# Order of the last attention group in a fused macaron block: values first, then maximum and weights, and a closing one step later

## The chip, the core and the metric

The kernel runs on one NeuronCore of a Trainium2 chip. The metric is device time in microseconds (us) of one execution; the time of a kernel is the median of its runs. The engines are named as in the profile: PE is TensorE (matmul; PEld its weight loads), DVE is VectorE, ACT is ScalarE, POOL is GpSimd, SP is SyncE. Each engine takes its own instructions in order, and waits on semaphores for the others.

## The reference

The input `x` is 2 x 2048 tokens of 256 numbers, float32. Three sublayers follow each other, each on a layer norm of `x`:

```
x = x + 0.5 * ffn(layernorm(x))
x = x + attn(layernorm(x))
x = x + 0.5 * ffn(layernorm(x))

ffn(x):  silu(q(x) @ q(w_gate).T) * (q(x) @ q(w_up).T)  ->  q(h) @ q(w_down).T      # hidden 704
attn(x): scores = (qr kr + qi ki) / sqrt(256);  softmax;  weights @ vr, weights @ vi;  @ Wo.T + bo
```

`q` rounds to a 4-bit grid in blocks of 16 numbers. The attention has one head; queries, keys and values are 512 wide (a real and an imaginary part of 256).

## The kernel before, in words

The 4096 tokens are 32 tiles of 128. The kernel folds the attention's matrices when it starts (`wa` from Wq and Wk, `wvo` from Wv and Wo), so that scores are a product of normed tokens with `uT = wa * normed tokens`, and the values' product is weights times normed tokens, followed by `wvo`.

**Attention** (`attention`, L660 to L903) works on 8 groups of 4 query tiles (512 queries, `Q`), 4 groups for each of the 2 batches. A group goes through 8 steps (`NP`), each for a pair of key tiles. One loop (L873) counts steps `n` over all groups, and in each step three groups are at work:

- the scores of group `gi` (`scores`, L701): PE writes `ps`, ACT copies it to a piece `st` (128 x 1024), DVE keeps the running maximum `most`; `peak` (L724) turns it on PE (`pm`) and reduces it on DVE to `mx` in the group's last step;
- the weights of the group ahead: `highest` (L734) spreads `mx` over the partitions, with four transposes on PE (`pb`) and a copy on ACT to `top`; `weights` (L741) subtracts `top` from a piece on DVE (L743), takes exp on ACT (L744) and, in the last group, adds the piece to `sums` on POOL (L750, L753);
- the values of the group that is 8 + 2 steps behind (`LAG` is 2): `values` (L776). Groups 0 to 6 use seven half-size products instead of eight: PE writes seven quarters `m` in two PSUM tiles (L805), with right sides that DVE has added up (`tw`, L764 to L768). The last group, number 7, takes the plain way: 4 matmuls of 512 columns a step into `z` (L783).

When a group's values are complete, `totals` (L833) transposes the sums of its weights on PE (`pl`) and takes their reciprocals on DVE (L842, L843); `collect` (L815) puts the seven quarters together into `zT`, with a copy on ACT (L824) and seven adds on DVE (L825 to L831), which also frees the two PSUM tiles of `m`; `close` (L850) multiplies `zT` by `wvo` on PE (`poa`, L856) and adds the result to `x` on DVE (L864). `closing` carries a group from `collect` to a later step's `close`.

**The second FFN** starts while attention ends. It is a generator (`ffn`) of which the loop at L935 takes one turn after some steps of attention, from step 66 on after each. A turn computes a tile's gate and up products (`gu`, L428, 8 matmuls of 352 columns, in PSUM tiles out of the same two buffers `p_big` as the seven quarters `m`), Silu on ACT (L442), and their product on DVE (L446); later turns round the result, transpose it (`th`, L463) and multiply it by the down matrix (`po`, L472).

No order is written out by hand at this place. Each engine's order comes from a planner, which starts from the order in which the code issues and may place an instruction ahead of one that it expects to wait. So a moved call shifts what stands near it, and can change what else is put between.

Steps 64 to 73 of the loop have no scores left: they hold the weights of group 7 (steps 64 to 71), the last two steps of values of group 6 (steps 64 and 65), and the values of group 7 (steps 66 to 73).

Of the kernel before, what the change touches and what calls it, by code (L numbers as in the profile page):

```python
# [52 lines left out]
def kernel(ctx: ExitStack, tc: tile.TileContext, x, wqT, bq, wkT, bk, wvT, bv, woT, bo,  # L53
# [539 lines left out]
    NP = tiles // 2  # L593
    LAG = 2
    RING = NP // 2 + LAG
    groups = NT // QG
# [63 lines left out]
    def attention(batches, at, kt, late):  # L660
# [15 lines left out]
        def queries(gi):  # L676
            gr = Group()
            gr.i = gi
            b, k = divmod(gi, tiles // QG)
            gr.of = batches[b]  # L680
            gr.uT = kt.tile([P, KD, Q], FP, tag="uT", name=f"uT{gi}", bufs=2)
            for c in range(KD):
                ps = p_t.tile([P, 2, HQ], FP, tag="t", name=f"pu{gi}_{c}")
                for h in range(2):
                    for kc in range(KD):
                        nc.tensor.matmul(  # L686
                            out=ps[:, h, :],
                            lhsT=wa[:, kc, ts(c, P)],
                            rhs=gr.of.xT[2 * k + h][:, kc, :, :].rearrange("p v t -> p (v t)"),
                            start=(kc == 0),  # L690
                            stop=(kc == KD - 1),
                        )
                nc.scalar.activation(
                    gr.uT[:, c, :], ps.rearrange("p h q -> p (h q)"), AF.Identity, bias=wkbq[:, c:c + 1]
                )
            gr.rc = at.tile([P, QG], FP, tag="rc", name=f"rcg{gi}", bufs=2)
            nc.vector.tensor_scalar(gr.rc, gr.of.rc[:, ts(k, QG)], bqbk, None, ALU.add)
            gr.pieces = []
            return gr

        def scores(gr, s):  # L701
            n = gr.i * NP + s
            pool = at if n // RING % 2 == 0 else late["pool"]
            piece = pool.tile([P, 2, Q], FP, tag="st", name=f"st{gr.i}_{s}", bufs=RING)
            for v in range(2):
                ps = p_acc.tile([P, Q], FP, tag="acc", name=f"ps{gr.i}_{s}_{v}")
                for c in range(KD):
                    scored = nc.tensor.matmul(  # L708
                        out=ps,
                        lhsT=gr.of.xT[s][:, c, v, :],  # L710
                        rhs=gr.uT[:, c, :],
                        start=(c == 0),
                        stop=(c == KD - 1),
                    )
                nc.scalar.copy(piece[:, v, :], ps)  # L715
                if s == 0 and v == 1:
                    gr.most = at.tile([P, Q], FP, tag="most", name=f"most{gr.i}")
                    seen = nc.vector.tensor_tensor(gr.most, ps, piece[:, 0, :], ALU.max)
                elif s > 0:
                    seen = nc.vector.tensor_tensor(gr.most, ps, gr.most, ALU.max)  # L720
            gr.pieces.append(piece)
            return seen.ins, scored.ins
# [11 lines left out]
        def highest(gr):  # L734
            pt = p_t.tile([P, QG, P], FP, tag="t", name=f"pb{gr.i}")
            for u in range(QG):
                nc.tensor.transpose(pt[:, u, :], gr.mx[:, u:u + 1].to_broadcast([P, P]), ident)
            gr.top = late["pool"].tile([P, Q], FP, tag="top", name=f"top{gr.i}")
            nc.scalar.copy(gr.top, pt.rearrange("p u s -> p (u s)"))  # L739

        def weights(gr, s):  # L741
            piece = gr.pieces[s]
            nc.vector.tensor_tensor(piece, piece, gr.top.unsqueeze(1).to_broadcast([P, 2, Q]), ALU.subtract)  # L743
            nc.scalar.activation(piece, piece, AF.Exp, scale=SCALE)  # L744
            if s == 0:
                gr.sums = late["pool"].tile([P, 2, HQ], FP, tag="sums", name=f"sums{gr.i}")
            if not seven(gr):
                both = piece.rearrange("p v (h q) -> p v h q", h=2)
                if s == 0:
                    add(gr.sums, both[:, 0, :, :], both[:, 1, :, :], ALU.add)  # L750
                else:
                    for v in range(2):
                        add(gr.sums, gr.sums, both[:, v, :, :], ALU.add)  # L753

        def seven(gr):
            return gr.i < groups - 1

        def sums_of_weights(gr, s):


            piece = gr.pieces[s]
            b = piece.rearrange("p v (h q) -> p (v h) q", h=2)
            t = late["pool"].tile([P, 4, HQ], FP, tag="tw", name=f"tw{gr.i}_{s}", bufs=2)
            nc.vector.tensor_tensor(  # L764
                t[:, 0:2, :], b[:, 0:4:3, :], b[:, 1:2, :].to_broadcast([P, 2, HQ]), ALU.add
            )
            nc.vector.tensor_tensor(t[:, 3, :], t[:, 1, :], b[:, 0, :], ALU.add)  # L767
            nc.vector.tensor_tensor(t[:, 2, :], t[:, 3, :], b[:, 2, :], ALU.add)  # L768
            if s == 0:
                gr.first = t  # L770
            else:
                add(gr.sums, t[:, 1:3, :], gr.first[:, 1:3, :] if s == 1 else gr.sums, ALU.add)  # L772
                gr.first = None
            gr.t[s] = t
# [40 lines left out]
        def collect(gr):  # L815
            gr.zT = late["pool"].tile([P, KD, Q], FP, tag="zT", name=f"zT{gr.i}")
            if not seven(gr):
                for c in range(KD):
                    nc.scalar.copy(gr.zT[:, c, :], gr.z[c])  # L819
                return  # L820
            m1, m6, m2, m7, m5, m3, m4 = gr.m
            u = late["pool"].tile([P, 3, HQ], FP, tag="u", name=f"u{gr.i}")
            vadd = nc.vector.tensor_tensor
            nc.scalar.copy(u[:, 0, :], m1)  # L824
            vadd(u[:, 1, :], m6, u[:, 0, :], ALU.add)  # L825
            vadd(gr.zT[:, 0, 0:HQ], m2, u[:, 0, :], ALU.add)
            vadd(u[:, 2, :], m7, u[:, 1, :], ALU.add)
            vadd(gr.zT[:, 1, HQ:Q], m5, u[:, 2, :], ALU.subtract)
            vadd(u[:, 1, :], m5, u[:, 1, :], ALU.subtract)
            vadd(gr.zT[:, 0, HQ:Q], m3, u[:, 1, :], ALU.add)  # L830
            vadd(gr.zT[:, 1, 0:HQ], m4, u[:, 2, :], ALU.add)  # L831
# [13 lines left out]
        def residual(gr):  # L845
            g, j = divmod(gr.i * QG, GT)
            gr.xo = xs[g][:, j:j + QG, :]
            nc.gpsimd.tensor_tensor(gr.xo, gr.xo, bout.unsqueeze(1).to_broadcast([P, QG, D]), ALU.add)

        def close(gr):  # L850
            xo = gr.xo
            for u0 in range(0, QG, 2):
# [10 lines left out]
                for u in range(u0, u0 + 2):  # L863
                    nc.vector.scalar_tensor_tensor(  # L864
                        xo[:, u, :], po[:, u - u0, :], gr.rs[:, u:u + 1], xo[:, u, :], ALU.mult, ALU.add
                    )

        def behind(seen):
            return tc.issue_after(seen) if seen is not None else nullcontext()

        todo = {0: queries(0)}
        closing = None
        for n in range(groups * NP + NP + LAG):  # L873
            gi, s = divmod(n, NP)
            seen, scored = scores(todo[gi], s) if gi < groups else (None, None)
            with behind(seen):
                if s == 0 and 0 < gi <= groups:
                    todo[gi - 1].t = {}
                    highest(todo[gi - 1])
                    weights(todo[gi - 1], 0)  # L880
                if s + 1 < NP and 0 < gi <= groups:
                    weights(todo[gi - 1], s + 1)
                if s == NP // 2 and gi + 1 < groups:
                    todo[gi + 1] = queries(gi + 1)
                gv, sv = divmod(n + 1 - NP - LAG, NP)
                if 0 <= gv < groups and seven(todo[gv]):
                    sums_of_weights(todo[gv], sv)
                if n >= NP + LAG:
                    gv, sv = divmod(n - NP - LAG, NP)
                    values(todo[gv], sv)  # L890
                    if closing is not None:
                        close(closing)
                        closing = None
                    if sv == LAG:
                        residual(todo[gv])
                    if sv == NP - 1:
                        closing = todo.pop(gv)
                        totals(closing)
                        collect(closing)
                if s == NP - 1 and gi < groups:  # L900
                    peak(todo[gi])
            yield seen, scored
# [11 lines left out]
    late = {}  # L914
    batches = [Batch(b) for b in range(NB)]
    att = attention(batches, at, kt, late)
    begun = 0
    done = 0
# [82 lines left out]
```

## Time and profile before

| | us |
|---|---|
| median of 3 runs | 1074.61 (1074.57 to 1074.98) |
| the profiled execution, its own time | 1073.74 |
| its span in the profile | 1071.9 |
| PE busy | 1044.7 (97% of the span) |
| DVE busy | 805.8 (75%) |
| ACT busy | 469.9 (44%) |
| POOL busy | 253.6 (24%) |
| L783, the values of the last group, first to last start | 769.2 to 837.5 |
| granted PE clock | 1.0 |

The profile's times are counted from the start of the span. A row of the timeline has start, duration, engine, line, operation, tiles written and read, sizes, how many instructions are merged in it, and in brackets the idle time of the engine before it and what ended it. A matmul in float32 shows as two rows of PE (x8 for four matmuls); a transpose as one.

### The profile page before, as it was taken

To read this page: it belongs to the slowest core of one execution; us is meant where nothing else is said; L and a number is where in the kernel's file an instruction comes from. 1 tells how busy PE (TensorE), PEld (TensorE's weight loads), DVE (VectorE), ACT (ScalarE), POOL (GpSimd) and SP (SyncE) were. 2 spreads that over 40 slices of the span, in tenths; PEclk is the share of its full clock that TensorE was granted. 3 is DMA by queue.
4 is the path that set the end of the run, shared out by engine and by line. 5 is a ranking of instruction groups with operands and counts; after the bars stand their busy time and mean duration, and the time that the engine had idled before them with its cause. 6 is when DMAs were issued, how large, how long until landed. Compare 5 with 4: busy or idle time off the path is not lost.

```text
span 1071.9 us, 11329 instructions
## 1 busy us (share of the span) xinstructions
PE 1044.7 (97%) x4206; PEld 731.6 (68%) x4206; DVE 805.8 (75%) x1387; ACT 469.9 (44%) x739; POOL 253.6 (24%) x148
## 2 busy tenths in 40 slices
PE   6998999999999999999999999999999999999998
PEld 5676777777775666676675666666655777777776
DVE  7999998867634888576688958678767587777575
ACT  4754654544335735447343633343333244343232
POOL 4563121210103020111124111212461021221110
PEclk9999999999999999999999999999999999999999
DMA  9000000000000000000000000000000000000001
GB/s 321 1 1 1 1 1 1 1 1 1 0 1 1 1 1 0 1 1 1 0 1 1 1 0 1 1 1 1 0 1 1 10 20 10 20 10 20 20 10 40
DMA packets 7286, 13.50 MB, mean 13 GB/s; under 512 B 1344, under 2 KB 3648, under 8 KB 6848
## 3 DMA queue, kind: packets, MB, share of 16 engines
q1 hardware_dynamic: 6128, 12.13, 3.1%
q10 hardware_dynamic: 1104, 0.66, 0.3%
q8 instruction: 33, 0.54, 0.2%
q14 instruction: 21, 0.17, 0.1%
HBM read 8.59 MB, written 4.19 MB: 12 GB/s over the span
## 4 chain that ended last, share of the span: by engine, by line
PE 89%; DVE 7%; ACT 2%; DMA 1%; issue 1%; POOL 0%; SPq 0%; DVEq 0%; ACTq 0%; POOLq 0%
PE gu L428 26%; PE ps L708 19%; PE m L805 15%; PE po L472 14%; PE th L463 4%; PE poa L856 3%; PE pu L686 2%; PE z L783 2%; PE tx L403 1%; DVE st L743 1%; PE wm L338 1%; PE txa L624 1%; ACT xn L234 1%; DVE h L285 1%; DVE h L283 1%
## 5 line engine op out<-in xcount | busy, mean ns | idle before, releaser
L428 PE MATMUL gu<-wgu,xqT 128*128 128x352 f32 x1024 | 317.9, 460 | 3.0 <-DVE h L446 2.7
L428 PEld LDWEIGHTS gu<-wgu,xqT 128*128 128x128 f32 x1024 | 188.4, 190 | 97.6 <-DVE h L446 3.8
L708 PE MATMUL ps<-uT,xT 128*128 128x512 f32 x512 | 232.2, 593 | 0.7 <-DVE most L720 0.7
L472 PE MATMUL po<-wd,hqT 128*128 128x256 f32 x768 | 176.1, 379 | 0.0
L472 PEld LDWEIGHTS po<-wd,hqT 128*128 128x128 f32 x768 | 144.7, 190 | 28.2 <-ACT zT L819 0.6
L708 PEld LDWEIGHTS ps<-uT,xT 128*128 128x128 f32 x512 | 95.1, 190 | 93.2 <-issue 81.0
L720 DVE TENSOR_TENSOR most<-ps,most 128x512 f32<-128x512 f32 x112 | 77.0, 688 | 93.5 <-ACT st L715 92.8
L184 POOL TENSOR_TENSOR h<-h,qh_s 128x1408 f32<-128x1408 f32 x26 | 67.5, 2595 | 294.0 <-DVE h L182 252.1
L715 ACT COPY st<-ps 128x512 f32<-128x512 f32 x128 | 74.5, 583 | 134.1 <-PE ps L708 133.5
L805 PE MATMUL m<-tw,xn 128*128 128x256 f32 x448 | 124.9, 380 | 0.0
L464 ACT COPY hqT<-th 128x512 f32<-128x512 f32 (+1 forms) x128 | 55.4, 481 | 156.7 <-PE th L463 154.5
L772 POOL TENSOR_TENSOR sums<-tw,sums 128x512 f32<-128x512 f32 x42 | 56.9, 1354 | 232.3 <-DVE tw L768 212.9
L744 ACT ACTIVATE st<-st 128x1024 f32<-128x1024 f32 x64 | 67.5, 1057 | 76.0 <-DVE st L743 75.6
L805 PE MATMUL m<-st,xn 128*128 128x256 f32 x336 | 100.0, 379 | 0.0
L446 DVE TENSOR_TENSOR h<-h,gu 128x704 f32<-128x704 f32 x64 | 56.3, 879 | 55.5 <-PE gu L428 52.8
L805 PEld LDWEIGHTS m<-tw,xn 128*128 128x128 f32 x448 | 84.8, 190 | 13.1 <-DVE tw L767 1.2
L743 DVE TENSOR_TENSOR st<-st,top 128x1024 f32<-128x1024 f32 x64 | 83.2, 1312 | 0.8 <-ACT top L739 0.8
L805 PEld LDWEIGHTS m<-st,xn 128*128 128x128 f32 x336 | 63.2, 190 | 26.2 <-issue 19.4
L180 DVE SCALAR_TENSOR_TENSOR h<-qh_m,h 128x1408 f32<-128x1408 f32 (+1 forms) x30 | 45.8, 1527 | 33.1 <-ACT qh_m L179 32.9
L442 ACT ACTIVATE h<-gu 128x704 f32<-128x704 f32 x64 | 48.2, 753 | 44.9 <-PE gu L428 44.6
L179 ACT ACTIVATE qh_m<-h 128x1408 f32<-128x1408 f32 (+1 forms) x30 | 38.9, 1297 | 45.9 <-DVE h L170 42.1
L463 PE MATMUL th<-ident,h 128*128 128x128 f32 x384 | 53.1, 273 | 1.4 <-ACT hqT L464 1.4
(175 smaller groups left out, 1262.5 us busy)
## 6 DMA issues: line engine op xcount, KB each, us to landing
out_dram<-x SPq DMA_DIRECT2D x15, 256.0 KB, 2.1
x<-in_x_dram SPq DMA_DIRECT2D x3, 1024.0 KB, 13.1
n_down<-in_w_down_dram SPq DMA_DIRECT2D x1, 704.0 KB, 9.6
n_up<-in_w_up_dram SPq DMA_DIRECT2D x1, 640.0 KB, 6.2
x<-in_x_dram ACTq DMA_DIRECT2D x1, 512.0 KB, 5.4
wq_sb<-in_wqT_dram SPq DMA_DIRECT2D x1, 512.0 KB, 6.8
wk_sb<-in_wkT_dram SPq DMA_DIRECT2D x1, 512.0 KB, 4.5
wv_sb<-in_wvT_dram SPq DMA_DIRECT2D x1, 512.0 KB, 6.8
```

Source lines behind the costliest of these rows:

```text
L184: last.tensor_tensor(yb, yb, scale.unsqueeze(2).to_broadcast([P, nb, BLK]), ALU.mult)
L428: nc.tensor.matmul(out=ps[:, b2, 0:HALF], lhsT=xqT[:, i % XT, kc, :], rhs=wgu[:, kc, ts(which * 2 + b2, HALF)], start=(kc == 0), stop=(kc ...
L446: nc.vector.tensor_tensor(h, h, up, ALU.mult)
L463: nc.tensor.transpose(ps[:, r - r0, :], hq[:, chunk(r)], ident)
L472: nc.tensor.matmul(out=po, lhsT=hqT[:, r, :], rhs=wd[:, r, :], start=(r == 0), stop=(r == NR - 1))
L708: scored = nc.tensor.matmul(out=ps, lhsT=gr.of.xT[s][:, c, v, :], rhs=gr.uT[:, c, :], start=(c == 0), stop=(c == KD - 1),)
L715: nc.scalar.copy(piece[:, v, :], ps)
L720: seen = nc.vector.tensor_tensor(gr.most, ps, gr.most, ALU.max)
L743: nc.vector.tensor_tensor(piece, piece, gr.top.unsqueeze(1).to_broadcast([P, 2, Q]), ALU.subtract)
L744: nc.scalar.activation(piece, piece, AF.Exp, scale=SCALE)
L772: add(gr.sums, t[:, 1:3, :], gr.first[:, 1:3, :] if s == 1 else gr.sums, ALU.add)
L805: i = nc.tensor.matmul(out=gr.m[k], lhsT=left, rhs=right, start=first, stop=last)
```

## The change

Two things change in the loop at L873, for the steps behind the last group's scores (`gi == groups`, steps 64 to 71). First, `highest` and `weights` of group 7 are issued at the end of the step, behind the values (and, in step 65, behind `totals` and `collect`) of group 6, and no longer at its beginning. Second, `close` of group 6 is held until step 67 (`s > LAG`); before, it came in step 66. For all other groups the order stays.

```
+        def shifted(gr, s):
+            if s == 0:
+                gr.t = {}
+                highest(gr)
+                weights(gr, 0)
+            if s + 1 < NP:
+                weights(gr, s + 1)
...
             with behind(seen):
-                if s == 0 and 0 < gi <= groups:
-                    todo[gi - 1].t = {}
-                    highest(todo[gi - 1])
-                    weights(todo[gi - 1], 0)
-                if s + 1 < NP and 0 < gi <= groups:
-                    weights(todo[gi - 1], s + 1)
+                if 0 < gi < groups:
+                    shifted(todo[gi - 1], s)
...
                     values(todo[gv], sv)
-                    if closing is not None:
+
+                    if closing is not None and (gi < groups or s > LAG):
                         close(closing)
                         closing = None
...
                         collect(closing)
+                if gi == groups:
+
+                    shifted(todo[gi - 1], s)
```

In the built programs every engine has the same instructions before and after. Only their order differs, at the following places; step numbers are those of the values.

| engine | before | after |
|---|---|---|
| PE | five of the seven `m` of step 6, `pb`, the other two, the seven of step 7 | all seven `m` of step 6, `pb`, the seven of step 7 |
| PE | `pl`, `z` step 0, one `poa`, two `gu` of tile 0, seven `poa`, six `gu` of tile 0, `z` step 1, `gu` of tile 1 | `pl`, `z` step 0, eight `gu` of tile 0, `z` step 1, eight `poa`, `gu` of tile 1 |
| DVE | L743 pieces 0, 1, 2; L825, L826, L842, L827, L843; piece 3; L828, L829; piece 4; L830, L831; pieces 5, 6; four L864; piece 7; L201; L446 | L743 pieces 0, 1; L825, L826, L842, L827, L843; piece 2; L828, L829; piece 3; L830, L831; pieces 4, 5, 6; L446; piece 7; four L864 with L201 and L204 between |
| ACT | `top`, exp 0, L824, exp 1 to 6, table load and Silu (L442) of tile 0, table load, exp 7 | `top`, L824, exp 0 to 3, table load and Silu of tile 0, table load, exp 4 to 7 |

POOL and SP keep their order.

## The prediction

> **What bounds the kernel now.** I read the page's busy line and its chain first, then who PE waited for behind 755 us (the stage that the change touches and all that follows), then the timeline of each engine between 762 and 778 us.
>
> ```profile
> PE 1044.7 (97%) x4206; PEld 731.6 (68%) x4206; DVE 805.8 (75%) x1387; ACT 469.9 (44%) x739; POOL 253.6 (24%) x148
> ...
> PE 89%; DVE 7%; ACT 2%; DMA 1%; issue 1%; POOL 0%; SPq 0%; DVEq 0%; ACTq 0%; POOLq 0%
> ```
>
> PE is the bound: busy 97%, and 89% of the chain. So an edit is worth what it takes out of PE's waits. Its waits from 755 us to the end:
>
> ```profile
> PE poa L856 <- DVE zT L830: 1.5, 1, 1.5
> PE pb L737 <- DVE mx L732: 0.7, 1, 0.7
> PE th L463 <- ACT hqT L464: 0.5, 1, 0.5
> ```
>
> Only 2.7 us, and the first two, 2.2 us, lie where the change is. PE's timeline shows both:
>
> ```profile
> 762.76 1.03 PE L805 MATMUL m<-tw,xn 128*128 128x256 f32 x4
> 764.51 0.65 PE L737 MATMUL pb<-ident,mx 128*128 128x128 f32 x4 [0.72 <-DVE mx L732]
> 765.00 0.60 PE L805 MATMUL m<-st,xn 128*128 128x256 f32 x2
> 765.43 0.59 PE L805 MATMUL m<-tw,xn 128*128 128x256 f32 x2
> 765.86 0.59 PE L805 MATMUL m<-st,xn 128*128 128x256 f32 x2
> ...
> 768.88 0.60 PE L840 MATMUL pl<-ident,sums 128*128 128x128 f32 x4
> 769.32 3.60 PE L783 MATMUL z<-st,xn 128*128 128x512 f32 x8
> 772.76 0.59 PE L856 MATMUL poa<-wvo,zT 128*128 128x256 f32 x2
> 773.19 1.35 PE L428 MATMUL gu<-wgu,xqT 128*128 128x352 f32 x4
> 776.03 3.26 PE L856 MATMUL poa<-wvo,zT 128*128 128x256 f32 x14 [1.50 <-DVE zT L830]
> ```
>
> Matmul ends overlap the next start, so I count from start to start. Rows of 256 columns follow each other every 0.216 us (765.00 to 765.43 holds two), of 352 every 0.297, of 512 every 0.43. Four rows from 762.76 leave PE free at 763.63; pb starts at 764.51: **0.88 us lost**, more than the 0.72 printed. Four gu rows from 773.19 leave it free at 774.38; poa starts at 776.03: **1.65 us lost**.
>
> **The change part by part.** No operation is added or removed, no DMA moves, SP's and POOL's orders stay. What moves is the order on PE, DVE and ACT, which the built programs give.
>
> *The way to the maximum.* mx is ready at 764.45 (L732). In the new order PE has two more matmuls of values (4 x 0.216 = 0.86 us) ahead of pb: from 763.63 to 764.49. pb then starts at 764.51 as before, but the last seven products begin at 764.51 + 0.49 = 765.00 and not at 765.86. Gain **0.86 us**. top stays where it was, and so does the first L743 (766.17), behind L836.
>
> *The first values.* pl comes at 768.02, z of step 0 could start at 768.46. It needs exp 0, which ended at 768.48 before; L824 now stands ahead of it on ACT, but waits only for the fourth of the last seven products (end about 766.9, copy done by 767.3), so exp 0 keeps its start of 767.43. z starts at about 768.55: **0.1 us lost**.
>
> *The closing.* gu of tile 0 now follows z step 0 (8 rows x 0.43 = 3.44): 771.99 to 774.37 for the gate half (8 x 0.297), then the up half; z step 1; then poa. zT is long complete by then, so the 1.65 us go. But a wait comes in their place: the up half writes the second PSUM tile of m, which L828 to L831 must have read. Before, they had until 780; now they have until **774.37**. Queued behind that wait on PE are all the matmuls of tile 0's up half, z step 1, the closing and so on: every us of it counts in full.
>
> *When does L831 end?* Two pieces instead of three stand ahead of L825 on DVE. L743 starts at 766.17 and 767.31, L825 at 768.45 (1.14 each), and the rows below give 771.26 - 769.58 = 1.68 us from L825 to the next L743, which is then piece 2, at **770.12**.
>
> ```profile
> 769.58 0.42 DVE L825 TENSOR_TENSOR u<-m,u 128x256 f32<-128x256 f32 x1
> ...
> 771.17 0.17 DVE L843 RECIPROCAL rs<-rs 128x4 f32<-128x4 f32 x1
> 771.26 2.08 DVE L743 TENSOR_TENSOR st<-st,top 128x1024 f32<-128x1024 f32 x1
> ```
>
> ```profile
> 769.63 1.28 POOL L750 TENSOR_TENSOR sums<-st 128x512 f32<-128x512 f32 x1 [3.84 <-PE pl L840]
> 770.99 1.27 POOL L753 TENSOR_TENSOR sums<-sums,st 128x512 f32<-128x512 f32 x1
> ```
>
> L743 takes 1.22 us alone; this one took 2.08: it could not begin its work until POOL's L753 was done at 772.25, and ended 1.08 later. The next L753 (asked for at 772.33) took 2.14: it in turn ended 1.14 after that L743. DVE's adds that read PSUM (0.41 throughout) are not held up. POOL's first L750 is released by pl, so it moves forward with PE by 0.86: 768.77, and the first L753 to **770.13**. The two meet within 0.01 us[...].
>
> - DVE first: piece 2 ends at 771.34, L828 and L829 follow, piece 3 asks at 771.92 and is held by L753 to 772.48, ends at 773.56; L830, L831 end at 774.22, visible to PE some 0.06 later (764.45 to 764.51 above): 774.28. PE arrives at 774.37, or 774.47 with the 0.1 of z. **No wait.**
> - POOL first: L753 to 771.39, piece 2 ends 772.47, piece 3 (held by the second L753 to 773.61) 774.69, L831 at 775.35: PE waits **about 0.95 us**.
>
> [...] The trace has a finer answer: of close pairs, DVE was not held where its start was only 0.015 us behind POOL's (L285 at 50.00, POOL's L287 at 49.98), and was held from 0.060 on. I take DVE first. By the one the sum is 0.86 + 1.65 - 0.1 = **2.4 us gained**, by the other 1.45.
>
> *ACT.* The table loads of Silu and exp (1.28 us each in the trace) and Silu move ahead of exp 4. [...] z step 4 is due at 804, exp 4 done by about 779 by the row[...]. Tile 0's Silu is done near 776.6, its bank is due for tile 1's gate at 783.5.
>
> *DVE behind it.* Pieces 4 to 6 alternate with POOL, 1.08 + 1.14 = 2.2 us each: from L831's 774.2 piece 4 ends at 775.8 (its L753 is already halfway), piece 5 at 778.0, piece 6 at 780.2. L446 of tile 0 (0.86 us) falls behind them and ends at about 781, or 782 with POOL first; the bank that it frees is due at 785.8. L864 runs 3 us later; no one waits for it before the rounding of tile 24's tokens. From 786 on, orders are the same, PE waits for nothing but 0.2 us pieces and the 0.5 at th, and all of it hangs on PE's own output, so it moves along. Uncovered cost of these edits: nothing; if their cover went, it would be us for us.
>
> **Sum.** Profiled execution 1073.74 - 2.4 = 1071.3, span 1069.5. The runs' median lies 0.87 above the profiled one, and I keep that distance: 1074.61 - 2.4 = **1072.2 us**.
>
> **The rivals.**
> A: [...] the new wait of 0.95 us at gu's up half takes the place of part of the old one: 1074.61 - 1.45 = 1073.15. For it: the start times tie, and pb, if it loses the 0.05 us that its first row spent on a late weight load, brings POOL forward by just that. Against it: the near pairs above.
> B: *Freed time is lost later* on PE: 1074.3 or so. Against it: PE has hardly a wait left after 786, and what it waits for there comes from PE itself.
> C, slower: *DVE's queue becomes the bound* between 770 and 786. L828 to L831, and then L446, stand behind five pieces[...]. The longest L743 took 2.51 us, 1.29 over its own time: with both ahead of L831 so held, L831 ends near 776.4, PE waits 1.9 and still gains 0.5. It decides only from an L831 end of 776.9 on, or where L446 ends after 785.8 + 2.5; for 0.2% (2.15 us) slower, 779.0 or 790.5. The profile has no row that long; I keep it for what one profile can't show: 1076.8.
> D: *The edit does nothing* is ruled out by the order as built: pb and poa stand elsewhere.
>
> **How the numbers follow.** DVE first 0.58, A 0.29, B 0.08, C 0.05. About 0.2%, 2.15 us, is what a measurement of this kernel can tell from no change. My forecast lies just beyond it, 0.25 us away; I give seven eighths of its chance to that side: faster 0.51, same 0.44 (the rest, A and B), slower 0.05. The range runs from the whole of both waits and 0.4 us for the spread of runs (the three before span 0.41) below, 1071.7, to A and 0.5 us above, 1073.7; B, C and the tails stay outside.
>
> **What would show it.** Right: pb starts at 764.5 with no idle before it; z step 0 near 768.5; poa after z step 1 with no wait; PE's wait for DVE at gu's up half under 0.1 us; tile 1's gu starting at 783.6 rather than 786.1. A is seen in the first L753 of 1.27 us with piece 2's L743 at 2.3, and a PE wait at gu for L831 of about 0.95. Wrong: a wait of PE of over 1.5 us between 768 and 786, or PE waits behind 786 that sum to more than 2 us.

## The result and the profile after

The changed kernel takes 1071.64 us (median of 12 runs, 1071.30 to 1072.46); the kernel before, timed beside it, 1074.49 us (12 runs, 1073.74 to 1074.98). The ratio is 0.9976, 95% interval 0.9968 to 0.9984: 2.85 us less, some 1.7 to 3.4. The forecast was 1072.2 us and 2.4 us less; the median lies 0.06 us below the low end of its range. The kernel before also came out 0.12 us lower than in the three runs that the forecast starts from; as a gain, 2.85 us lies inside the range, which allows 0.9 to 2.9.

The profiled execution took 1072.21 us, its span is 1070.4 us. The list of PE's waits from 755 us to the end, in the changed kernel, has one line:

```profile
PE th L463 <- ACT hqT L464: 0.5, 1, 0.5
```

Both waits that stood ahead of this line before, at poa and at pb, are gone, and the list has none in their place (it doesn't show a loss of 0.18 us at z, which the account of the prediction comes back to). The page has PE busy 98% of the span and 91% of the chain. PE's timeline in the stretch of the change:

```profile
763.67 1.03 PE L805 MATMUL m<-tw,xn 128*128 128x256 f32 x4
764.53 0.59 PE L805 MATMUL m<-st,xn 128*128 128x256 f32 x2
764.97 0.59 PE L805 MATMUL m<-tw,xn 128*128 128x256 f32 x2
765.42 0.65 PE L737 MATMUL pb<-ident,mx 128*128 128x128 f32 x4
765.90 0.60 PE L805 MATMUL m<-st,xn 128*128 128x256 f32 x2
...
768.93 0.60 PE L840 MATMUL pl<-ident,sums 128*128 128x128 f32 x4
769.44 3.70 PE L783 MATMUL z<-st,xn 128*128 128x512 f32 x8
772.98 4.90 PE L428 MATMUL gu<-wgu,xqT 128*128 128x352 f32 x16
777.72 3.60 PE L783 MATMUL z<-st,xn 128*128 128x512 f32 x8
781.15 3.62 PE L856 MATMUL poa<-wvo,zT 128*128 128x256 f32 x16
784.60 4.90 PE L428 MATMUL gu<-wgu,xqT 128*128 128x352 f32 x16
```

The two products that stood behind pb now fill the wait for mx; the eight gu of tile 0 run in one go; poa comes behind the second z and waits for nothing. The kernel before, from behind poa to tile 1's gate, which the prediction doesn't show:

```profile
779.13 3.71 PE L428 MATMUL gu<-wgu,xqT 128*128 128x352 f32 x12
...
786.11 4.90 PE L428 MATMUL gu<-wgu,xqT 128*128 128x352 f32 x16
```

I measure the gain from start to start on PE, from the start of the last of the four rows ahead of the change (762.76 + 0.65 = 763.41 before, 763.67 + 0.65 = 764.32 after) to tile 1's gate (786.11 before, 784.60 after): 22.70 us before, 20.28 after, **2.42 us less**. From tile 1's gate to PE's last row it is 282.00 us in both: nothing is won or lost behind.

The spans differ by only 1.5 us, because this execution had lost 0.9 us more before the stretch began (763.67 against 762.76 for the same row). That is not the change: see the last section.

DVE's timeline, with the first L753 of POOL below it:

```profile
770.95 0.17 DVE L843 RECIPROCAL rs<-rs 128x4 f32<-128x4 f32 x1
771.03 1.19 DVE L743 TENSOR_TENSOR st<-st,top 128x1024 f32<-128x1024 f32 x1
772.14 0.41 DVE L828 TENSOR_TENSOR zT<-m,u 128x256 f32<-128x256 f32 x1
772.47 0.41 DVE L829 TENSOR_TENSOR u<-m,u 128x256 f32<-128x256 f32 x1
772.80 1.64 DVE L743 TENSOR_TENSOR st<-st,top 128x1024 f32<-128x1024 f32 x1
774.37 0.41 DVE L830 TENSOR_TENSOR zT<-m,u 128x256 f32<-128x256 f32 x1
774.70 0.41 DVE L831 TENSOR_TENSOR zT<-m,u 128x256 f32<-128x256 f32 x1
```

```profile
771.03 2.33 POOL L753 TENSOR_TENSOR sums<-sums,st 128x512 f32<-128x512 f32 x1
```

L743 of piece 2 and POOL's L753 both start at 771.03. The subtraction took 1.19 us, and POOL's addition 2.33 instead of the 1.27 of the kernel before (its row at 770.99). L831 ends at 775.11; PE needs it at 772.98 + 2.38 = 775.36, when the gate half of tile 0 (8 rows) is through and the up half, which writes the PSUM tile that L831 reads, begins.

### The profile page after: what moved, and what is told of

Read it like the earlier page. It is cut to its first block, busy times and chain, and to the rows that moved or that the text cites. A ratio compares the mean times of both kernels' runs of the same rounds, so it can differ in the third digit from the quotient of the medians.

```text
span 1070.4 us, 11326 instructions
## 1 busy us (share of the span) xinstructions
PE 1047.0 (98%) x4206; PEld 733.0 (68%) x4206; DVE 805.9 (75%) x1387; ACT 470.0 (44%) x739; POOL 255.9 (24%) x148
## 4 chain that ended last, share of the span: by engine, by line
PE 91%; DVE 5%; ACT 2%; DMA 1%; issue 0%; POOL 0%; ACTq 0%; DVEq 0%; POOLq 0%
PE gu L428 26%; PE ps L708 19%; PE m L805 15%; PE po L472 14%; PE th L463 4%; PE poa L856 3%; PE z L783 3%; PE pu L686 2%; PE tx L403 1%; PE wm L338 1%; PE txa L624 1%; ACT xn L234 1%; DVE h L285 1%; DMA n_gate<-in_w_gate_dram 1%; DVE h L283 1%
## 5 line engine op out<-in xcount | busy, mean ns | idle before, releaser
L446 DVE TENSOR_TENSOR h<-h,gu 128x704 f32<-128x704 f32 x64 | 56.3, 879 | 53.3 <-PE gu L428 50.6
L743 DVE TENSOR_TENSOR st<-st,top 128x1024 f32<-128x1024 f32 x64 | 82.8, 1305 | 0.8 <-ACT top L739 0.8
L442 ACT ACTIVATE h<-gu 128x704 f32<-128x704 f32 x64 | 48.2, 753 | 44.7 <-PE gu L428 44.6
```

The lines of the kernel that those rows point to most:

```text
L446: nc.vector.tensor_tensor(h, h, up, ALU.mult)
```

## The experiments

Each is timed beside the kernel before, on the same chip. "Stretch" is the time on PE defined above; 22.70 us before, 20.28 after.

| kernel | median, us | before beside it, us | ratio, 95% interval | stretch, us |
|---|---|---|---|---|
| changed (first time) | 1071.64 | 1074.49 | 0.9976 (0.9968 to 0.9984) | 20.28 |
| changed_again | 1071.67 | 1074.31 | 0.9976 (0.9966 to 0.9986) | 20.28 |
| values_first_only | 1072.09 | 1074.43 | 0.9981 (0.9972 to 0.9989) | 20.68 |
| closing_later_only | 1074.14 | 1074.43 | 0.9997 (0.9989 to 1.0005) | 22.22 |
| before_no_sums | 1073.16 | 1074.43 | 0.9987 (0.9981 to 0.9994) | 21.39 |
| pool_first | 1072.30 | 1074.43 | 0.9980 (0.9973 to 0.9987) | 20.28 |
| pool_first_forced | 1071.69 | 1074.31 | 0.9975 (0.9967 to 0.9983) | 20.29 |
| pool_first_by_more | 1073.03 | 1073.91 | 0.9989 (0.9981 to 0.9998) | 21.36 |
| adds_ahead_of_piece | 1071.81 | 1074.31 | 0.9979 (0.9971 to 0.9988) | 20.28 |
| closing_two_later | 1071.89 | 1074.31 | 0.9978 (0.9969 to 0.9987) | see below |

Runs of one kernel scatter by 1.1 to 2.1 us, so medians tell differences of half a microsecond badly. The stretch is read from one profile each, but it came out within 0.01 us in the five profiles in which PE has the same order and no wait; I go by it, and use the medians to see that nothing contradicts it.

### One half at a time

The first half alone (values_first_only), the edit against the changed kernel:

```
-                    if closing is not None and (gi < groups or s > LAG):
+                    if closing is not None:
```

> The first half of the change alone: in the last group's steps the maximum and the weights come behind the values, but the closing of group 6 stays in step 66. My account (two separate PE waits are taken away): pb's 0.88 us go; poa is still met early, and waits for L830, which now has two subtractions of pieces ahead of it instead of three or four. With DVE ahead of POOL at piece 2, L830 ends near 773.9 and PE, free at 773.6, waits some 0.35 us (if POOL is ahead, 1.4). Gain against before 2.1 us (1.0 with POOL ahead), so about 1072.4. Rival (all of the gain at the closing comes from its being a step later): PE still loses the whole 1.65 us at poa and the gain is 0.8 us, 1073.7.

Measured: stretch 20.68 us, 2.02 less than before. PE in this kernel:

```profile
772.01 0.59 PE L856 MATMUL poa<-wvo,zT 128*128 128x256 f32 x2
772.45 1.35 PE L428 MATMUL gu<-wgu,xqT 128*128 128x352 f32 x4
773.96 3.26 PE L856 MATMUL poa<-wvo,zT 128*128 128x256 f32 x14 [0.17 <-DVE zT L830]
```

pb's wait is gone, and so is most of the one at poa. The four gu rows leave PE free at 772.45 + 1.19 = 773.64, so 0.32 us are left of 1.65; the expectation had 0.35. The closing's delay was not needed for the larger part of the gain: with the weights issued behind the values, one piece fewer stands ahead of L830 on DVE.

The second half alone (closing_later_only), the edit against the kernel before:

```
-                    if closing is not None:
+                    if closing is not None and (gi < groups or s > LAG):
```

> The second half alone: only the closing of group 6 comes a step later, the maximum and the weights stay ahead of the values. My account: pb still costs its 0.88 us. On DVE three and four pieces still stand ahead of L825 and L830, so L831 ends at 776.2 as before; PE comes to the up half of tile 0 (which needs L831) at 775.1 and waits 1.0 to 1.1 us there in place of 1.65 at poa. Gain about 0.6 us, 1073.9. Rival (the delay alone hides the whole wait): no wait between pl and tile 1's gate, gain 1.65 us, 1072.8.

Measured: stretch 22.22 us, 0.48 less. PE in this kernel:

```profile
773.62 2.53 PE L428 MATMUL gu<-wgu,xqT 128*128 128x352 f32 x8
777.14 2.63 PE L428 MATMUL gu<-wgu,xqT 128*128 128x352 f32 x8 [0.98 <-DVE zT L831]
```

The wait for DVE has only changed its place: from poa, which reads zT, to the up half of tile 0, which writes the PSUM tile that L831 still reads. From 773.62 + 2.38 = 776.00 to 777.14 it costs 1.14 us. Here the same wait that the prediction weighed for the full change is real, since on DVE five pieces stand ahead of L831, and four in the changed kernel. (The two recorded expectations above count fewer pieces ahead of L830; DVE's rows have four with the first half alone, and five here and in the kernel before.) The interval of the times includes no change; they alone could not tell this gain from nothing.

### What the old wait was made of

before_no_sums is the kernel before without POOL's L753, so that the last group's sums hold piece 0 alone:

```
-                else:
-                    for v in range(2):
-                        add(gr.sums, gr.sums, both[:, v, :, :], ALU.add)
```

> The kernel before without the fourteen additions of POOL at L753: the sums of the last group's weights then hold piece 0 alone, so this group's softmax is not normed as the reference's. The order of all else stays. [...] My account: subtractions of pieces 3 and 4 take 1.2 us each instead of 2.08 and 1.63, L830 ends 1.3 us earlier, PE's wait at poa falls from 1.65 us to 0.2 to 0.4; pb's 0.88 stays. About 1074.49 - 1.3 = 1073.2. Rival (the wait at poa comes from the order on DVE[...]): the wait stays at 1.2 us or more.

Measured: stretch 21.39 us, 1.31 less. Its timeline of PE, and the two subtractions of DVE that had run beside L753 and taken longer:

```profile
774.99 3.26 PE L853 MATMUL poa<-wvo,zT 128*128 128x256 f32 x14 [0.19 <-DVE zT L827]
```

```profile
771.52 1.19 DVE L743 TENSOR_TENSOR st<-st,top 128x1024 f32<-128x1024 f32 x1
...
773.29 1.21 DVE L743 TENSOR_TENSOR st<-st,top 128x1024 f32<-128x1024 f32 x1
```

They took 2.08 us (the row is in the prediction) and 1.63 us in the kernel before:

```profile
773.92 1.63 DVE L743 TENSOR_TENSOR st<-st,top 128x1024 f32<-128x1024 f32 x1
```

Without L753 the two are 0.89 and 0.42 us shorter, so 1.3 of the 1.65 us at poa came with POOL's additions. The change itself brings one of the two back and leaves the other: the first subtraction behind the adds that begin at L825 takes 1.19 us for 2.08, the second still 1.64. And one piece fewer, 1.14 us, stands ahead of L830. Together that is what the rows show: L830 starts at 774.37 - 0.91 = 773.46 for 775.48 before, 2.02 us earlier (this execution is 0.91 us late up to the change).

### The tie with POOL's addition

The prediction rested its last 0.95 us on a tie. The first trial to turn it around failed: pool_first adds a small DVE operation that no other depends on, ahead of piece 2 in the code.

```
+            if gr.i == groups - 1 and s == 2:
+                spare = at.tile([P, 1], FP, tag="spare", name="spare")
+                nc.vector.tensor_scalar(spare, tiny, 1.0, None, ALU.mult)
             nc.vector.tensor_tensor(piece, piece, gr.top.unsqueeze(1).to_broadcast([P, 2, Q]), ALU.subtract)
```

> The changed kernel with one added operation of one column per partition on DVE just ahead of the subtraction of piece 2 (some 0.06 to 0.16 us)[...]. My account (the tie decides 0.95 us): piece 2's subtraction takes 2.2 to 2.4 us instead of 1.2, L831 ends at 775.3 or later, PE waits about 0.95 to 1.05 us at the up half of tile 0: 1071.64 + 1.0 = 1072.6. Rival (who is first does not matter to PE): no wait there, 1071.7.

The planner placed the operation where DVE was free, and it ran at 130.2 us. The kernel is the changed one in all that matters here (stretch 20.28 us), and says nothing of the tie. The second trial, pool_first_forced, ties the operation to its place in DVE's order, behind L843 of group 6 and ahead of piece 2, and keeps L828 behind piece 2 as in the changed kernel:

```
+            put = gr.i == groups - 1 and s == 2
+            if put:
+                spare = at.tile([P, 8], FP, tag="spare", name="spare")
+                put = nc.vector.reciprocal(spare, ones[:, 0:8])
+                queued_behind(put.ins, closing.rec.ins)
-            nc.vector.tensor_tensor(piece, piece, gr.top.unsqueeze(1).to_broadcast([P, 2, Q]), ALU.subtract)
+            sub = nc.vector.tensor_tensor(piece, piece, gr.top.unsqueeze(1).to_broadcast([P, 2, Q]), ALU.subtract)
+            if put:
+                queued_behind(sub.ins, put.ins)
+                queued_behind(closing.fifth.ins, sub.ins)
+            if gr.i == groups - 1 and s > 0:
+                queued_behind(sub.ins, gr.sub.ins)
+            gr.sub = sub
...
-            vadd(gr.zT[:, 1, HQ:Q], m5, u[:, 2, :], ALU.subtract)
+            gr.fifth = vadd(gr.zT[:, 1, HQ:Q], m5, u[:, 2, :], ALU.subtract)
...
-            nc.vector.reciprocal(gr.rs, gr.rs)
+            gr.rec = nc.vector.reciprocal(gr.rs, gr.rs)
```

> The changed kernel with one added reciprocal of 8 columns on DVE between L843 and the subtraction of piece 2, held at this place; all other orders are as in the changed kernel. [...] My account (the tie is worth 0.95 us): piece 2 takes 2.2 to 2.4 us, L831 ends 1.1 us later, PE waits 0.9 to 1.1 us at the up half of tile 0, and nothing gives it back: about 1 us over the changed kernel, 1072.7. Rival (PE has slack there): no wait, same time as the changed kernel.

It missed. In this kernel POOL's L753 stands at L764, and L743 at L748; the rows of POOL and DVE:

```profile
771.39 2.40 POOL L764 TENSOR_TENSOR sums<-sums,st 128x512 f32<-128x512 f32 x1
```

```profile
771.39 0.17 DVE L746 RECIPROCAL spare<-ones 128x8 f32<-128x8 f32 x1
771.48 1.18 DVE L748 TENSOR_TENSOR st<-st,top 128x1024 f32<-128x1024 f32 x1
```

POOL's addition starts 0.09 us ahead and is still the one that takes longer (2.40 us for 1.27; the subtraction takes 1.18). The stretch is 20.29 us. The third trial, pool_first_by_more, takes the reciprocal over 48 columns.

> As in the run before with the added reciprocal, but over 48 columns, so that the subtraction of piece 2 asks some 0.35 us behind POOL's first L753 and not 0.09, which still let DVE ahead. My account: [...] (a subtraction that began 0.27 us behind an L753 was held in the kernel before), piece 2 takes 1.9 to 2.1 us, L831 ends 1.1 us later than in the changed kernel, PE waits 0.9 to 1.1 us at the up half of tile 0 and nothing gives it back: 21.3 us from pb to tile 1's gate for 20.3, about 1072.7. If DVE is ahead even so, L831 is later by the 0.36 us of the reciprocal alone and the wait is 0.1 to 0.2 us. Rival (PE has slack there): no wait and 20.3 us.

```profile
771.02 1.27 POOL L764 TENSOR_TENSOR sums<-sums,st 128x512 f32<-128x512 f32 x1
```

```profile
771.02 0.42 DVE L746 RECIPROCAL spare<-ones 128x48 f32<-128x48 f32 x1
771.36 2.02 DVE L748 TENSOR_TENSOR st<-st,top 128x1024 f32<-128x1024 f32 x1
...
775.85 0.41 DVE L842 TENSOR_TENSOR zT<-m,u 128x256 f32<-128x256 f32 x1
```

```profile
772.97 2.53 PE L428 MATMUL gu<-wgu,xqT 128*128 128x352 f32 x8
776.31 2.63 PE L428 MATMUL gu<-wgu,xqT 128*128 128x352 f32 x8 [0.81 <-DVE zT L842]
```

Now POOL's addition takes 1.27 us and the subtraction 2.02, the last add ends at 776.26 instead of 775.11, and PE waits from 772.97 + 2.38 = 775.35 to 776.31: 0.96 us. The stretch is 21.36 us, 1.08 longer than the changed kernel's (the eight rows behind the wait take 0.1 us more than without one: 776.31 to 778.78 for 8 x 0.297), and the gain over the kernel before falls to 0.9 us in the medians (1.3 in the stretch). This is rival A of the prediction, made to happen.

adds_ahead_of_piece asks whether a longer subtraction costs PE anything by itself. It takes the reciprocal of group 6 over twice the columns, and in the planner's answer L828 and L829 stand ahead of piece 2, L830 and L831 ahead of piece 3:

```
-            nc.vector.reciprocal(gr.rs, gr.rs)
+            if gr.i == groups - 2:
+                wide = at.tile([P, QG, 2], FP, tag="wide", name="wide")
+                nc.vector.reciprocal(wide, gr.rs.unsqueeze(2).to_broadcast([P, QG, 2]))
+                gr.rs = wide[:, :, 0]
+            else:
+                nc.vector.reciprocal(gr.rs, gr.rs)
```

> The changed kernel with the reciprocal of group 6 taken over 8 columns instead of 4, to which the planner answers by placing L828 and L829 ahead of the subtraction of piece 2, and L830 and L831 ahead of that of piece 3; PE, ACT and POOL keep their orders. [...] My account (what costs is a late L831[...]): piece 2 takes 1.8 to 2.2 us, but L831 ends a us earlier than in the changed kernel with all its pieces behind it, PE waits nowhere, the time is the changed kernel's, 1071.6 to 1072.0. Rival [...]: 1072.7.

```profile
771.10 1.65 DVE L743 TENSOR_TENSOR st<-st,top 128x1024 f32<-128x1024 f32 x1
772.68 0.41 DVE L830 TENSOR_TENSOR zT<-m,u 128x256 f32<-128x256 f32 x1
773.01 0.41 DVE L831 TENSOR_TENSOR zT<-m,u 128x256 f32<-128x256 f32 x1
```

Here too the subtraction took longer (1.65 us; POOL's L753, at 770.40, 1.27), and the stretch is 20.28 us all the same: L831 ended at 773.42, 1.3 us before PE needed it (gu starts at 772.34, its up half 2.38 later, at 774.72). What costs is a late L831, not the longer subtraction. This order has the changed kernel's time and 1.3 us of slack where that has 0.25; it is not measurably faster, since PE had no wait left to take away.

### A repeat, and a closing later still

> The changed kernel once more, beside the three variants below. My account: from the last product ahead of pb to tile 1's gate PE takes 2.4 us less than in the kernel before (20.3 us for 22.7)[...], and the time is 1071.6 to 1072.0. What lies over 2.4 us in the difference of the medians is scatter from the opening of the kernel[...]. Rival [...]: a piece 2 of 2.2 us or more in this profile, and 21.3 us.

The repeat has the same stretch to 0.01 us, again 1.19 us for the subtraction of piece 2 beside 2.33 for POOL's addition, and 1071.67 us.

```
-                    if closing is not None and (gi < groups or s > LAG):
+                    if closing is not None and (gi < groups or s > LAG + 1):
```

> The changed kernel with the closing of group 6 held one step more, to step 68. My account: PE has no wait left between pb and tile 1's gate, so there is nothing more to win; L446 of tile 1 and the rounding of tiles 0 and 1 come a little earlier on DVE, no PE wait follows: same time as the changed kernel. Rival (the later the closing the better): a further 0.2 us or more.

With poa behind tile 1's products the stretch does not end at the same work, so I take it to PE's last row: 302.27 us, against 302.28 in the changed kernel. Nothing more is won, as expected.

## Why the prediction was right, and where it was off

**The way to the maximum** (0.86 us): right. pb starts with no idle time printed before it, and the rows between are as worked out.

**z step 0** (0.1 us lost): the place is right, the size is 0.18 us. z starts 0.51 us behind pl, where transposes of four rows need 0.44, and its second row then follows 0.54 us behind the first, for 0.43 in the kernel before. The cause named, exp 0, shows in 0.15 us that the first weight load of z waits; the second wait has no releaser in the profile, and the kernel before has 0.24 us there too:

```profile
769.44 0.30 PEld L783 LDWEIGHTS z<-st,xn 128*128 128x128 f32 x2 [0.15 <-ACT st L744]
769.98 0.19 PEld L783 LDWEIGHTS z<-st,xn 128*128 128x128 f32 x1 [0.24 <-issue]
```

**The closing** (1.65 us): right. No wait is left there, because L831 ends 0.25 us ahead of PE's need, or 0.20 with the 0.05 that pass from an end on DVE to the start on PE (776.26 to 776.31 in pool_first_by_more) taken off; the prediction had 0.09, or 0.19 with z's delay. closing_later_only and pool_first_by_more show the wait that stands there when L831 is late, 1.14 and 0.96 us, where the prediction had priced it at 0.95. The term is worth a little more than forecast: from poa's first row, or gu's now, to tile 1's gate PE takes 786.11 - 772.76 = 13.35 us before and 784.60 - 772.98 = 11.62 after, 1.73 less. The fourteen rows behind the old wait had taken 3.10 us (776.03 to 779.13) where 14 x 0.216 is 3.02.

**The tie**: the outcome was right (piece 2 in 1.19 us), and the two start times agreed to 0.01 us as forecast. Of the reason, half holds. From near pairs of the kernel before I read that an operation of DVE keeps its length when it starts 0.015 us behind POOL's (L285 at 50.00: 0.88 us), and is longer from 0.060 on (L697 at 333.51: 2.33 us, where its median is 0.22). The first half covers this tie; the second does not hold for L743, which in pool_first_forced started 0.09 us behind and took 1.18. The longer ones that I used were small operations of DVE (L697 with 4 columns, L658 with 128). With L743 0.27 us behind an L753 it took 2.08 (the kernel before); what happens between 0.09 and 0.27 is not shown. So A was less likely than the 0.29 given: in pool_first_forced L743 kept its length 0.09 us behind POOL, and five profiles with this order and no added delay, the changed kernel's among them, all have piece 2 in 1.19 or 1.20 us.

**ACT and DVE behind it**: right. Tile 0's Silu ends at 777.7, its L446 at 781.9, each well ahead of its need; from tile 1's gate on, PE's time is the same to 0.01 us. Rivals B and C have nothing to show.

**The sum**: 2.4 us forecast, 2.42 in the stretch. That it agrees to 0.02 us is luck in part: z cost 0.08 us more than forecast and the closing was worth 0.08 more (0.86 - 0.18 + 1.73 = 2.41). The difference of the medians, 2.85 us in the first timing and 2.64 in the second, is a little larger; both lie beyond the 2.15 us that the prediction takes as the least it can tell, and both intervals reach below it. That the rest is scatter is not shown. The record gives every run's mean granted clock, 1.000 in some and 0.998 in others; in the second timing the medians of runs with the same clock are 1073.68 (9 runs before) and 1071.30 (2 after), and 1074.41 (24) and 1072.01 (7): 2.38 and 2.40 us less.

## What to carry to other kernels

When PE is busy all the time, look for its few waits and ask what else it could be doing there: two products of 0.43 us each, moved ahead of pb, filled a wait that no faster producer was needed for. A wait that is moved away from its reader can come back at the next writer of the same buffer, here the up half that reuses the PSUM tile (1.14 us in closing_later_only), so follow the last reader (L831) to its new deadline. And where operations of two engines take longer beside each other (here 2.08 us for 1.19 on DVE, 2.33 for 1.27 on POOL), compute both start times after the shift: what moves one engine's release moves its overlaps too.

## What the runs showed of the hardware

**A subtraction beside POOL's addition.** Whose start stands first in the timeline did not decide which of the two took longer. With POOL's addition 0.09 us ahead (pool_first_forced), L743 took 1.18 us and the addition 2.40. With 0.27 (the kernel before) and 0.34 (pool_first_by_more), the addition took 1.27 us and L743 2.08 and 2.02. In the kernel before, beside a small DVE operation (L658, 128 columns), POOL's addition kept its 1.26 us with a lead of 0.10 (582.68 and 582.78), and L658 took 1.32, where its shortest is 0.28. The two cases differ in more than size: this L658 starts 0.04 us after the end of the operation ahead of it on DVE (582.46 + 0.28 = 582.74), L743 0.08 us before it (771.39 + 0.17 = 771.56 and 771.48). That gap alone does not decide either: L697 (333.51) took 2.33 us in the kernel before when it started 0.06 us behind POOL's L848 (333.45), and it began 0.08 us before the end of the operation ahead of it (332.90 + 0.69 = 333.59). What decides is not shown: a trace gives starts and lengths, so that a longer subtraction "could not begin its work until POOL's L753 was done" is the prediction's estimate from two ends 1.08 us apart.

**The opening.** Runs of one kernel differ by about 1 us and more. PE's timeline of the same 16 rows in the opening, first in the kernel before, then in the changed one:

```profile
13.58 4.65 PE L338 MATMUL wm<-e_k,e_q 128*128 128x256 f32 x16
```

```profile
13.48 5.73 PE L338 MATMUL wm<-e_k,e_q 128*128 128x256 f32 x16
```

The starts of these rows lie 0.43 us apart at first and 0.216 later; the last gap of 0.4 us or more ends at 15.69 us in the kernel before and at 17.75 in the changed one, and PE's next rows (L330) start 1.0 us later there (19.05 for 18.07), of which 0.9 us remain at 763 us. The granted clock is 1.00 in both traces from 13 to 19 us, and why the gaps differ is not shown. In values_first_only the 16 rows take 4.64 us, as in the kernel before.

The opening is not all of it: the mean granted clock of the profiled execution is 0.998 in nine of the eleven kernels, and 1.000 in the kernel before and in values_first_only. In the changed kernel's trace the granted clock is 0.84 from 99 to 100 us, 0.50 from 100 to 103 and 0.95 from 103 to 104; the kernel before has 1.00 throughout. Eight rows of gu there took 4.12 us (at 98.68) for 2.63 (at 97.73), and PE's wait for POOL behind them was 0.56 us for 2.04. PE's row behind that wait (L403) starts at 103.35 for 102.41, 0.94 us later than in the kernel before; the eight rows had started 0.95 later, so nothing was lost that lasted. Two profiled spans are therefore not to be compared whole when a change is worth 2 us; the stretch is.
